# A two-layer graph attention kernel: one weight sum loaded ahead of the next weights, and three products with attention vectors moved into the second product's stage

## The chip, the cores and the metric

The kernel runs on one core of a Trainium2 chip. The core has five engines with an instruction queue each: TensorE (PE, matrix products into PSUM; its weight loads are shown as PEld), VectorE (DVE), ScalarE (ACT), GpSimd (POOL) and SyncE (SP). In this kernel SP does no arithmetic, it issues DMA transfers; GpSimd issues the transfers that add to their destination. Every queue is worked off in the order in which it was written. The metric is the device time of one execution in microseconds; lower is better.

## The reference

The reference is two graph attention layers, a residual and a layer norm over 512 nodes with 768 features. The first layer has 8 heads of 768 features, the second has one. Cut to what matters:

```
def gat_layer(x, W, a_s, a_d, b, edge_index, concat):
    h = (x @ W).reshape(n, H, C)
    alpha_s = einsum('nhc,hc->nh', h, a_s)
    alpha_d = einsum('nhc,hc->nh', h, a_d)
    e = leaky_relu(alpha_s[src] + alpha_d[dst], 0.2)
    e = exp(e - segment_max(e, dst)[dst])
    alpha = e / (segment_sum(e, dst)[dst] + 1e-16)
    out = segment_sum(h[src] * alpha[:, :, None], dst)
    return out.reshape(n, H * C) + b

h = elu(gat_layer(x, W1, a_src1, a_dst1, b1, edges, True))     # 8 heads
out = layernorm(x + gat_layer(h, W2, a_src2, a_dst2, b2, edges, True))
```

## The kernel before, in words

The edge list becomes a 512 x 512 matrix of edge counts at the start. From then on each head of the first layer is dense: a projection of x with the head's 768 x 768 weights, a softmax over the counted edges, a product of the attention matrix with the projected features, elu, and at once the head's share of the second layer's projection ("the second product"), which is added up over the heads.

The loop `for h in range(H - 1)` (line 991) runs in each round, in this order:

- `mixed(h, ...)` (line 867): the attention product of head h. TensorE's instructions have line 889.
- `second(h, GA, B2)` (line 442, called at 1011): the second product of head h, by a scheme of seven products P1 to P7 instead of eight, each in two halves. TensorE's line is 364, the evacuations on VectorE are L459. The loop over n from 2 to 6 (lines 1032 to 1072) puts the softmax of head h+1 between the halves: `lift` on ScalarE (L572), `leak` (L576) and `rank` (L581) on VectorE, `weigh` (L791 to L797) on VectorE, `turn_out` (a copy on ScalarE, L812, and a transposing DMA on SP, L814) and `turn_in` (L817).
- the projection of head h+2. For h from 1 to 5 it is `by_thirds` (line 407), which cuts the matrices in 2 x 3 and 3 x 3 blocks and needs 15 products P0 to P14 of eight TensorE instructions each instead of 18. TensorE's line is 423. The order of the products is P8, P13, P9, P2, P4, P12, P6, P0, P1, P10, P5, P14, P11, P7, P3.

The 15 products read sums of blocks of x and sums of blocks of weights. Nine of the sums of x lie in SBUF all the time. Five (for P7, P1, P6, P3 and P14) lie in gT, which the mixed product overwrites in each head; they are stored in DRAM once (`xd`), and `reload_x` (line 947, L948) brings them back in one transfer of 1280 KB at the end of each second product. P6 is the first product in the order that reads them.

The weight sums are made in two ways. `load_thirds` (line 132) loads the weights and lets GpSimd's adding transfers make some sums; its inner function `rest` (line 157), which the loop knows as `rest_of_thirds`, makes the others: VectorE operations (L165) and one pair of transfers for P11. P11's sum is a load on SP's queue (L161) into one half of the tile w2t4 and an adding transfer on GpSimd's queue (L162) on top of it, 256 KB each.

w2t4 and w2t2 are used twice in each round. Before `rest_of_thirds` they hold what `attended(h)` (line 975) loads for head h: 128 rows of the last head's W2 and the attention vectors of the second layer. It returns three VectorE operations (L985), products of these rows with the vectors, summed along the rows: 768, 384 and 384 elements wide. The first two read both tiles, the third only w2t2. They must be done before P11's load may write to w2t4.

`load_w2(h + 1)` (line 175, `load_w` at 103) loads the second product's next weights: seven transfers on SP's queue (L108, L116) and two adding ones on GpSimd's (L109, L120) into w1t1, w10 and w11. VectorE builds two more sums from them (`right`, L356 and L357); L356 is in VectorE's queue at the end of the 15 products.

The order of every queue is written out by hand: what stands first in the program is first in its engine's queue. A transfer on SP's queue that waits holds up everything behind it there.

Of the kernel before, what the change touches and what calls it, by code (L numbers as in the profile page):

```python
# [36 lines left out]
def gat_pass(  # L37
# [48 lines left out]
    def row_bcast(ap_row):  # L86
        return bass.AP(tensor=ap_row.tensor, offset=ap_row.offset, ap=[[0, P], [1, D]])
# [84 lines left out]
    def load_w1(h, slot="w2"):  # L172
        return load_w(W1, h, slot, w1[:, h * D:(h + 1) * D])

    def load_w2(h, slot="w1"):
        return load_w(W2, h, slot, w2[h * D:(h + 1) * D, :])

    def load_a(h, a_s, a_d):
        A[h] = []
        for name, a in (("a_s", a_s), ("a_d", a_d)):  # L180
            v = wpool.tile([P, D], F32, name=name)
            nc.sync.dma_start(v, row_bcast(a))
            A[h].append(v)
# [155 lines left out]
    def left(aT, s):  # L339
        a11, a12 = aT[:, :HK, :HN], aT[:, HK:, :HN]  # L340
        a21, a22 = aT[:, :HK, HN:], aT[:, HK:, HN:]
        tt = nc.vector.tensor_tensor
        return dict(P1=a11, P2=a12, P3=s[:, 2], P4=a22, P5=s[:, 0], P6=s[:, 1], P7=a21), [
            lambda: tt(s[:, 0], a21, a22, op=ALU.subtract),
            lambda: tt(s[:, 1], s[:, 0], a11, op=ALU.subtract),
            lambda: tt(a21, a11, a21, op=ALU.subtract),
            lambda: tt(s[:, 2], a12, s[:, 1], op=ALU.add),
        ]
# [23 lines left out]
    def half_logits(h, t):  # L372
        return [lambda al=al, a=a, sign=sign: nc.vector.scalar_tensor_tensor(
            scr, HS[h][:, t, :], sign, a, op0=ALU.mult, op1=ALU.mult, accum_out=al[:, t:t + 1])
            for al, a, sign in zip(AL[h], A[h], (1.0, -1.0))]
# [182 lines left out]
    def row_out(h):  # L558

        turned = small.tile([P, SQ], F32, name="turned", bufs=1)  # L560
        nc.vector.transpose(turned, wide[:, h % 2, :])
        row = drows.tile([NT, P], F32, name="drow")
        for j in range(P // SQ):
            nc.sync.dma_start(row[:, j * SQ:(j + 1) * SQ], turned[j * SQ:j * SQ + NT, :])
        BC[h] = qpool.tile([P, N], F32, name="q")
        r = row[:, :]
        nc.sync.dma_start(BC[h], bass.AP(tensor=r.tensor, offset=r.offset, ap=[[0, P], [1, N]]))
# [379 lines left out]
    def reload_x():  # L947
        nc.sync.dma_start(gF[:, :RELOAD * 2 * TH], stored)  # L948
# [42 lines left out]
    for h in range(H - 1):  # L991
        if 0 < h < H - 2:
            B3, rest_of_thirds = load_thirds(h + 2)
        elif h:
            A[H] = []
            for j, a in ((2, a_src2[0]), (4, a_dst2[0])):
                v = wpool.tile([P, HK, HALF], F32, name=f"w2t{j}").rearrange("p k n -> p (k n)")[:, :D]
                nc.sync.dma_start(v, row_bcast(a))
                A[H].append(v)
            last_sum = load_w2(H - 1, "w2")  # L1000
        GA, gsums = left(gT, gS)
        halves = [half_logits(h + 1, t) for t in ((0, 1) if h else (0, 1, 3))]
        besides[2:2] = [s_ for s_, _ in halves] + [lambda: row_out(h + 1)]
        finish = mixed(h, AA, BB, besides + [d_ for _, d_ in halves] + behind)
        besides, behind = [], []
        if h == 0:
            load_w1(2)()
        if h + 2 < H:
            load_a(h + 2, a_src1[h + 2], a_dst1[h + 2])
            attend = attended(h)  # L1010
        pairs = second(h, GA, B2)
        for m, _ in pairs[:2]:
            m()
        pairs[0][1]()
        for f in finish:
            f()
        gsums[0]()
        pairs[1][1]()
        gsums[1]()
        if pending:  # L1020
            pending.pop(0)()
        pairs[2][0]()
        gsums[2]()
        pairs[3][0]()
        gsums[3]()
        if pending:
            pending.pop(0)()
        pairs[2][1]()
        pairs[3][1]()
        last = h + 2 == H  # L1030
        q = [lift(h + 1, 0)]
        for n in range(2, 7):
            (m0, e0), (m1, e1) = pairs[2 * n:2 * n + 2]
            m0()
            if not last:
                m1()
            if n < 6:
                leak(q[n - 2])
                rank(q[n - 2], n - 2)
            if n < 5:  # L1040
                q.append(lift(h + 1, n - 1))
            if last:

                if n > 4:
                    turn_in(n - 5)
                if n == 6:
                    turn(q[2], 2)
                if n == 6:
                    weigh(q[3], 3)
                m1(lambda: turn(q[3], 3) if n == 6 else None)  # L1050
            if not last and n == 6:
                turn_in(0)
                weigh(q[2], 2)
                turn_out(q[2], 2)
            e0()
            if last and 2 < n < 6:
                weigh(q[n - 3], n - 3)
                if n < 5:
                    turn_out(q[n - 3], n - 3)
            if not last and 3 < n < 6:  # L1060
                weigh(q[n - 4], n - 4)
                turn_out(q[n - 4], n - 4)
            if not last and n == 6:
                weigh(q[3], 3)
                turn_out(q[3], 3)
                if 0 < h:
                    reload_x()
                load_w2(h + 1)()
            e1()
            for f in in_second[:1]:  # L1070
                f()
            del in_second[:1]
        if 0 < h and h + 2 < H:
            for f in attend:
                f()
            sums = rest_of_thirds()
            pairs = by_thirds(h + 2, XB, B3)
            AA, sums3 = left_sums(h + 1)
            B2, sums2 = right(W2[h + 1], "w1")
            for n in range(15):  # L1080
                pairs[n][0]()
                for p in {0: ("P6", "P2"), 1: ("P4",), 4: ("P10",), 5: ("P0",), 6: ("P1",), 9: ("P7",),
                          12: ("P3",)}.get(n, ()):
                    sums[p]()
                if n == 5:
                    BB, rsums_ = right_sums()
                    sums3 += rsums_
                if n in (2, 3, 5, 6, 8, 9, 10):
                    for _ in range(2 if n == 8 else 1):
                        sums3.pop(0)()  # L1090
                if n in (11, 13):
                    logits(h + 2, HS[h + 2], 2 + (n - 11) // 2)
                if n == 14:
                    sums2[0]()
                    behind = sums2[1:]
                pairs[n][1]()
                if n in (1, 2, 4):
                    turn_in((n + 2) // 2)
            assert not sums3
        elif h + 2 < H:  # L1100
            B_, sums = right(W1[h + 2], "w2")
            pairs = projection(h + 2, XA, B_)
            for n in range(14):
                pairs[n][0]()
                if n == 0:
                    for f in attend:
                        f()
                    B2, sums2 = right(W2[h + 1], "w1")
                if n in (1, 3):
                    sums[n // 2]()  # L1110
                if n == 1:
                    AA, sums3 = left_sums(h + 1)
                pairs[n][1]()
                if n in (1, 2, 4):
                    turn_in((n + 2) // 2)
                if n == 5:
                    BB, sums3 = right_sums()
                if 1 <= n < 9:
                    sums3.pop(0)()
                if n == 0:  # L1120
                    XB, early, again_, store, late_ = x_thirds()
                if n in (2, 4, 6, 8, 9):
                    early.pop(0)()
                if n == 9:
                    store()
                if n == 9:
                    again_()
                if n == 12:
                    late_.pop(0)()
                    sums2.pop(0)()  # L1130
                    behind = sums2 + late_[:2]
                    in_second = late_[2:]
                if n in (11, 13):
                    logits(h + 2, HS[h + 2], 2 + (n - 11) // 2)
        else:
            last_sum()
            B2, sums2 = right(W2[H - 1], "w1")
# [162 lines left out]
```

## Time and profile before

| | |
|---|---|
| median of 3 runs | 676.59 us (674.71 to 676.74) |
| the profiled execution | 677.39 us, its span 675.6 us |
| mean granted TensorE clock | 0.973 |
| DMA moved | 109.87 MB, mean 163 GB/s |
| TensorE, VectorE, ScalarE, GpSimd busy | 641.9, 537.9, 289.9, 63.6 us |

The profile is one execution, taken by the hardware profiler. Its times run from the span's start. A line such as L423 is the kernel's line of an instruction; the tile names stand without their buffer numbers, so w2t is w2t1, w2t2 or w2t4, and w is w10 or w11. "SPq" and "POOLq" are the queues that issue transfers. A row of the instructions in order of time has the start, the duration, engine, line, operation, output and input tiles, shapes and a count, and in brackets how long the engine stood idle before it and what ended that. Durations of TensorE's rows overlap a little with the next start, since its instructions are pipelined. A row of a table by stretches has the stretch, its length, the engine's busy time with the number of instructions, the clock granted to TensorE as a share of full speed, the mean busy share of the DMA engines and the GB/s they moved.

### The profile page before, as it was taken

Reading aid. Unit: us, or ns where it says so; the run is one execution under the profiler, and the core shown is the slowest. Engines: PE = TensorE matmul, PEld = TensorE weight load, DVE = VectorE, ACT = ScalarE, POOL = GpSimd, SP = SyncE. Lnnn points to the kernel's source line nnn. Section 1 sums busy time; section 2 is a strip of 40 time slices with the busy share of each in tenths; the row PEclk is TensorE's granted clock in tenths of the full one; section 3 lists DMA queues with packets and bytes.
Section 4 is the critical chain, followed back from the end, with each engine's and each line's share of the span. In section 5 each row is a group of like instructions: output and inputs, shape, how many; then the busy total and the mean of one; then the engine's idle time right before and its main releaser. Section 6 shows DMA issues by size and latency. Waiting matters only on the chain.

```text
span 675.6 us, 7677 instructions
## 1 busy us (share of the span) xinstructions
PE 641.9 (95%) x2509; PEld 445.3 (66%) x2509; DVE 537.9 (80%) x1162; ACT 289.9 (43%) x486; POOL 63.6 (9%) x105
## 2 busy tenths in 40 slices
PE   8999999999999799988999799997999889999996
PEld 5555685557668585777758686685857677544653
DVE  8989889979899578984889578885789758868685
ACT  5865564603544063611735035530636117443350
POOL 1300001012001020020200120010200210000000
PEclk9999999999999799997999899997999989999999
DMA  9993679697629483494907766294845955130031
GB/s 307 319 190 83 173 157 327 154 259 205 162 26 311 81 240 124 109 298 124 248 12 239 171 191 175 40 309 75 234 124 125 308 174 119 30 118 1 16 70 74
DMA packets 86844, 109.87 MB, mean 163 GB/s; under 512 B 40150, under 2 KB 67982, under 8 KB 86030
## 3 DMA queue, kind: packets, MB, share of 16 engines
q1 hardware_dynamic: 70590, 87.42, 40.9%
q0 software_dynamic: 15776, 21.30, 19.1%
q10 hardware_dynamic: 432, 0.59, 0.3%
q8 instruction: 22, 0.36, 0.2%
q14 instruction: 24, 0.20, 0.1%
HBM read 95.12 MB, written 2.90 MB: 145 GB/s over the span
## 4 chain that ended last, share of the span: by engine, by line
PE 86%; DMA 8%; DVE 2%; issue 1%; ACT 1%; SPq 0%; DVEq 0%; POOLq 0%; ACTq 0%
PE mm L364 41%; PE mm L889 18%; PE mm L423 14%; DMA w2t<-in_L_gnn_W_dram 7%; PE mm L835 3%; PE mm L1246 3%; PE held L364 2%; DMA gT<-xd 2%; PE tr L664 1%; PE held L544 1%; PE bc L233 1%; PE bc L664 0%; DVE scr L379 0%; ACT os L636 0%; PE mm L262 0%
## 5 line engine op out<-in xcount | busy, mean ns | idle before, releaser
L364 PE MATMUL mm<-w,gT 128*128 128x384 f32 x252 | 83.6, 486 | 0.0
L429 ACT ACTIVATE hs<-mm 128x512 f32<-128x512 f32 x30 | 17.9, 597 | 128.3 <-PE mm L423 110.3
L364 PEld LDWEIGHTS mm<-w,gT 128*128 128x128 f32 x252 | 47.9, 190 | 31.9
L431 DVE TENSOR_TENSOR hs<-hs,mm 128x512 f32<-128x512 f32 x45 | 30.8, 685 | 43.4 <-PE mm L423 43.3
L583 ACT ACTIVATE q<-q,nmax 128x512 f32<-128x512 f32 x36 | 25.8, 721 | 89.5 <-DVE nmax L581 89.5
L889 PE MATMUL mm<-PT,hs 128*128 128x256 f32 x252 | 61.3, 379 | 0.0
L364 PE MATMUL mm<-w1t,gS 128*128 128x384 f32 x180 | 60.6, 487 | 0.0
L423 PE MATMUL mm<-w2t,xS 128*128 128x256 f32 x120 | 37.7, 469 | 23.1 <-DMA w2t<-in_L_gnn_W_dram 23.1
L889 PEld LDWEIGHTS mm<-PT,hs 128*128 128x128 f32 x252 | 47.8, 190 | 7.3 <-issue 0.4
L364 PEld LDWEIGHTS mm<-w1t,gS 128*128 128x128 f32 x180 | 34.1, 190 | 24.1 <-DVE w1t L356 0.5
L459 DVE TENSOR_TENSOR h<-h,mm 128x384 f32<-128x384 f32 x72 | 39.1, 550 | 12.0 <-PE mm L364 11.5
L423 PEld LDWEIGHTS mm<-w2t,xS 128*128 128x128 f32 x120 | 27.8, 236 | 29.7 <-issue 24.9
L889 PE MATMUL mm<-pS,gS 128*128 128x256 f32 x168 | 43.2, 380 | 0.0
L423 PE MATMUL mm<-w2r,gT 128*128 128x256 f32 x160 | 40.8, 407 | 0.0
L817 ACT COPY PT<-zr 128x1024 uint16<-128x1024 uint16 x34 | 39.3, 1156 | 2.6 <-DMA zr<-pS 1.9
L423 PE MATMUL mm<-w2r,xT 128*128 128x256 f32 x160 | 37.8, 379 | 0.0
L423 PEld LDWEIGHTS mm<-w2r,gT 128*128 128x128 f32 x160 | 33.8, 211 | 5.9
L889 PEld LDWEIGHTS mm<-pS,gS 128*128 128x128 f32 x168 | 31.8, 190 | 4.7 <-DVE pS L862 0.4
L109 POOL DMA_DIRECT2D w1t<-in_L_gnn_W_dram x7 | 8.9, 1271 | 272.0 <-DVE hs L852 130.7
L812 ACT COPY pS<-q 128x1024 uint16<-128x1024 uint16 x26 | 27.2, 1044 | 17.0 <-DVE q L797 17.0
L423 PEld LDWEIGHTS mm<-w2r,xT 128*128 128x128 f32 x160 | 30.4, 190 | 5.2
L364 PE MATMUL mm<-w1t,gT 128*128 128x384 f32 x96 | 32.3, 486 | 0.0
(233 smaller groups left out, 1268.7 us busy)
## 6 DMA issues: line engine op xcount, KB each, us to landing
w2r<-in_L_gnn_W_dram SPq DMA_DIRECT2D x48, 384.0 KB, 8.9
w<-in_L_gnn_W_dram SPq DMA_DIRECT2D x43, 384.0 KB, 10.0
gT<-xd SPq DMA_DIRECT2D x5, 1280.0 KB
w1t<-in_L_gnn_W_dram SPq DMA_DIRECT2D x9, 576.0 KB
w<-in_L_gnn_W_dram POOLq DMA_DIRECT2D x8, 576.0 KB, 9.5
w1t<-in_L_gnn_W_dram POOLq DMA_DIRECT2D x7, 576.0 KB, 9.6
w2t<-in_L_gnn_W_dram SPq DMA_DIRECT2D x15, 256.0 KB, 7.5
w2t<-in_L_gnn_W_dram POOLq DMA_DIRECT2D x15, 256.0 KB, 8.9
```

The source lines that it names most:

```text
L109: nc.gpsimd.dma_start(t1, upper[:, :, R], accum_op=ALU.add)
L364: nc.tensor.matmul(ps[:, :HALF], A_[p][:, k, i * P:(i + 1) * P], B_[p][:, k, :], start=start and k == 0, stop=k == HK - 1, skip_group_chec ...
L423: nc.tensor.matmul(bank[chain][:, i * TH:(i + 1) * TH], A_[p][:, k, i * P:(i + 1) * P], B_[p][:, k, :], start=first and i == k == 0, stop= ...
L429: nc.scalar.activation(out(o), ps, AF.Copy, scale=how)
L431: nc.vector.tensor_tensor(out(o), out(o), ps, op=how)
L459: nc.vector.tensor_tensor(a, a, ps, op=ALU.subtract if p == "P7" else ALU.add)
L583: nc.scalar.activation(q, q, AF.Exp, bias=nmax, scale=-1.0)
L812: nc.scalar.copy(apart.rearrange("p (h n) -> p h n", h=2), q.bitcast(U16).rearrange("p (n h) -> p h n", h=2))
L817: nc.scalar.copy(PT.rearrange("p s n -> p (s n)").bitcast(U16).rearrange("p (s n h) -> p s n h", s=NT, h=2)[:, :, t * P:(t + 1) * P, :], p ...
L835: nc.tensor.matmul(ps[:, :N], HS[h][:, s, c * P:(c + 1) * P], PT[:, s, :], start=(s == 0), stop=(s == NT - 1))
L889: nc.tensor.matmul(bank[p][:, :HN], A_[p][:, k, c * P:(c + 1) * P], B_[p][:, k, :], start=over is None and k == 0, stop=k == 1, skip_group ...
L1246: nc.tensor.matmul(ps[:, :cols.stop - cols.start], PT[:, s, t * P:(t + 1) * P], h2[:, s, cols], start=(s == 2), stop=(s == 1))
```

## The change

Two things move, and both only for h from 1 to 5, the rounds with 15 products.

`rest_of_thirds()`, which issues P11's load on SP's queue and its adding transfer on GpSimd's and returns the VectorE sums, was called after the second product's loop. It is now called in the loop's last step (n = 6), after the last `turn_out` and before `reload_x()` and `load_w2(h + 1)`. The VectorE sums that it returns are placed as before.

The three operations of `attended(h)`, which were placed together after the loop, are now placed one each at the end of the steps n = 3, 4 and 5, behind the second evacuation `e1`.

```
                 turn_out(q[3], 3)
                 if 0 < h:
+                    sums = rest_of_thirds()
                     reload_x()
                 load_w2(h + 1)()
             e1()
             for f in in_second[:1]:
                 f()
             del in_second[:1]
+            if 0 < h and not last and 2 < n < 6:
+                attend[n - 3]()
         if 0 < h and h + 2 < H:
-            for f in attend:
-                f()
-            sums = rest_of_thirds()
             pairs = by_thirds(h + 2, XB, B3)
```

On SP's queue the order at the end of a second product was: four transposing transfers, the reload of gT (L948), seven weight loads (L108, L116), P11's load (L161). It is now: four transposing transfers, P11's load, the reload, the seven weight loads. On GpSimd's queue it was L109, L120, L162 and is now L162, L109, L120. TensorE's and ScalarE's queues are the same in both, and so are the number of instructions and the bytes.

## The prediction

> **What bounds the kernel now.** I read the page first (busy shares and the chain that ended last), then who waited for whom, then TensorE's instructions in order of time in one head.
>
> ```profile
> span 675.6 us, 7677 instructions
> PE 641.9 (95%) x2509; PEld 445.3 (66%) x2509; DVE 537.9 (80%) x1162; ACT 289.9 (43%) x486; POOL 63.6 (9%) x105
> ...
> PE 86%; DMA 8%; DVE 2%; issue 1%; ACT 1%; SPq 0%; DVEq 0%; POOLq 0%; ACTq 0%
> PE mm L364 41%; PE mm L889 18%; PE mm L423 14%; DMA w2t<-in_L_gnn_W_dram 7%; PE mm L835 3%; PE mm L1246 3%; PE held L364 2%; DMA gT<-xd 2%; PE tr L664 1%; PE held L544 1%; PE bc L233 1%; PE bc L664 0%; DVE scr L379 0%; ACT os L636 0%; PE mm L262 0%
> ```
>
> TensorE is busy 95% of the span and 86% of the chain. The only large item beside it is a transfer into w2t, the tile whose weight sum this change moves. The list of waits says how often TensorE really stands for it, and the rows of one head (the second of the five 15-product projections) say where; their columns are start and duration in us, and in brackets the idle time before.
>
> ```profile
> PE mm L423 <- DMA w2t<-in_L_gnn_W_dram: 23.1, 5, 4.9
> ```
>
> ```profile
> 297.76 1.89 PE L423 MATMUL mm<-w2r,xS 128*128 128x256 f32 x8
> 299.48 1.89 PE L423 MATMUL mm<-w2r,gT 128*128 128x256 f32 x8
> 305.80 3.75 PE L423 MATMUL mm<-w2t,xS 128*128 128x256 f32 x8 [4.43 <-DMA w2t<-in_L_gnn_W_dram]
> ...
> 313.66 1.03 PE L889 MATMUL mm<-PT,hs 128*128 128x256 f32 x4
> ```
>
> One product of eight matmuls normally starts 1.72 us after the one before (299.48 - 297.76). The 13th product, P11, comes at 305.80 instead of 301.21. It happens once in each of five heads. The second loss stands in the same rows: P11, P7 and P3 then take 7.86 us (305.80 to 313.66), where three pitches make 5.18. Stretches of these three products, first and last of the five and their sum (length, TensorE busy, granted clock, DMA share, GB/s):
>
> ```profile
> 227.03:235.02 7.99, 7.99 (x24) 0.65 0.00 0
> ...
> 542.21:549.63 7.42, 7.42 (x24) 0.70 0.30 74
> sum 38.76, PE 38.76; mean PE 7.75
> ```
>
> The granted clock is 0.65 to 0.70 there: the wait throttles TensorE, and it pays for that afterwards.
>
> **The change, part by part.** Removed, if P11's sum is there in time: the wait, 23.1 us plus five times the 0.16 by which a row's end overlaps the next start (1.89 - 1.73) = 23.9 us; and the slow clock, 38.76 - 5 x 5.18 = 12.9 us. Together 36.8 us, 7.4 a head. That is the most that it can bring.
>
> Is the sum in time? The two transfers of P11 (a load on SP's queue, then an adding one from GpSimd), and those around them:
>
> ```profile
> 280.95 1.05 ACT L812 COPY nr<-q 128x1024 uint16<-128x1024 uint16 x1 [0.88 <-DVE q L797]
> ```
> ```profile
> 282.02 1.23 SPq L814 DMA_TRANSPOSE zr<-nr  x1
> 283.36 0.52 SPq L948 DMA_DIRECT2D gT<-xd  x1
> 283.98 0.38 SPq L108 DMA_DIRECT2D w1t<-in_L_gnn_W_dram  x1
> 284.45 3.02 SPq L116 DMA_DIRECT2D w<-in_L_gnn_W_dram  x6
> 289.45 0.38 SPq L161 DMA_DIRECT2D w2t<-in_L_gnn_W_dram  x1
> ```
> ```profile
> 291.52 1.28 POOL L109 DMA_DIRECT2D w1t<-in_L_gnn_W_dram  x1 [42.47 <-PE mm L423]
> ...
> 301.25 1.22 POOL L162 DMA_DIRECT2D w2t<-in_L_gnn_W_dram  x1 [5.51 <-DVE hs L431]
> ```
> ```profile
> gT<-xd SPq DMA_DIRECT2D x5, 1280.0 KB
> w1t<-in_L_gnn_W_dram POOLq DMA_DIRECT2D x7, 576.0 KB, 9.6
> w2t<-in_L_gnn_W_dram SPq DMA_DIRECT2D x15, 256.0 KB, 7.5
> w2t<-in_L_gnn_W_dram POOLq DMA_DIRECT2D x15, 256.0 KB, 8.9
> ```
>
> Now P11's load is issued at 289.45, behind the reload and seven weight loads, and its add only at 301.25. In the changed order the load is the first thing behind the last transpose. Its issue time is the reload's old one plus whatever delays the transpose, at most the 2.07 us found below: 285.43. With the medians from issue to landing (7.5 and 8.9 us) the sum is there by 301.8, and P11 wants it at 301.21 plus whatever the product is delayed elsewhere (1.9 us, below). So even with the medians under load the wait goes; the load has less ahead of it, so I expect some 297.
>
> What moves on VectorE: the three products with attention vectors, 768, 384 and 384 wide.
>
> ```profile
> 269.08 0.56 DVE L459 TENSOR_TENSOR h<-h,mm 128x384 f32<-128x384 f32 x1 [1.38 <-PE mm L364]
> ...
> 281.30 0.95 DVE L985 SCALAR_TENSOR_TENSOR scr<-w2t,w2t 128x768 bf16<-128x768 f32 x1
> ...
> 282.29 0.56 DVE L985 SCALAR_TENSOR_TENSOR scr<-w2t,w2t 128x384 bf16<-128x384 f32 x1
> ...
> 282.78 0.55 DVE L985 SCALAR_TENSOR_TENSOR scr<-w2t 128x384 bf16<-128x384 f32 x1
> ...
> 283.37 0.69 DVE L165 TENSOR_TENSOR w2t<-w2r 128x512 f32<-128x512 f32 x1
> ```
> ```profile
> 269.55:283.37 13.82, 13.22 (x39) 1.00 0.32 60
> ```
>
> They take 281.30 to 283.37, 2.07 us. They go behind the evacuations of steps 3, 4 and 5 of the second product. VectorE's last wait for TensorE there ends at 269.08, and from 269.55 to 283.37 it is busy 13.22 of 13.82 us. So nothing absorbs them: the work behind each comes 1.0, 1.6 and 2.07 us later, while the weight sums from L165 on start when they do now. Banks and softmax steps have room, but the last weighing of q (L797) ends 2.07 us later, and behind it hang ScalarE's copy at 280.95, the transpose at 282.02 and all of SP's queue. That is the price: P11's load and then the reload of gT issue late.
>
> How much room has the reload? P11's load waits for the reload's landing today, so its issue time dates that landing; P6, the seventh product, is the first that reads the reloaded gT. First and last of the five heads, and the second:
>
> ```profile
> SPq L161 <- DMA gT<-xd: 8.8, 5, 1.9
> ```
> ```profile
> 211.06 0.38 SPq L161 DMA_DIRECT2D w2t<-in_L_gnn_W_dram  x1
> ```
> ```profile
> 211.85 1.89 PE L423 MATMUL mm<-w2t,gT 128*128 128x256 f32 x8
> ```
> ```profile
> 290.85 1.89 PE L423 MATMUL mm<-w2t,gT 128*128 128x256 f32 x8
> ```
> ```profile
> 525.13 0.39 SPq L161 DMA_DIRECT2D w2t<-in_L_gnn_W_dram  x1
> ```
> ```profile
> 526.78 1.89 PE L423 MATMUL mm<-w2t,gT 128*128 128x256 f32 x8
> ```
>
> The room is 0.79, 1.40 and 1.65 us; I use 1.2. Against it stand 2.07 us from VectorE, and P11's load ahead in the queue. That load costs at least its issue, 0.5 us (0.38 and a gap), and by its bytes a fifth of the reload's 6.1 us (289.45 - 283.36): 1.2. I take 1.0, nearer to the bytes since both go through one queue. So the reload lands 3.07 us later and P6 stands 1.9 us, 9.3 in five heads. The low bound is (2.07 + 0.5 - 1.2) x 5 = 6.8. P11's add (4.55 us from its issue at 301.25 to P11's start at 305.80) may also run beside the reload's end; at half rate for 1 to 2 us it adds up to 1 us a head, so the high bound is 14. Nothing below zero is possible there, because a load put ahead cannot bring the reload forward.
>
> Does this stall throttle TensorE too? Three stretches of 3.41 us: the one that ends where the clock fell in the fifth head, the one behind it, and one early in the kernel with a gap in which it did not fall:
>
> ```profile
> 536.39:539.80 3.41, 0.91 (x5) 1.00 1.12 254
> 539.80:543.21 3.41, 1.00 (x3) 0.50 0.46 72
> ```
> ```profile
> 14.13:17.54 3.41, 2.29 (x28) 1.00 1.06 386
> ```
>
> A stretch of 3.41 us with 0.91 us of work was followed by half clock; one with 2.29 us of work was not. A stall of 1.9 us leaves 1.5 us of work if it falls into one stretch, between the two. A fall costs what it costs now, 12.9/5 = 2.6 us; I put one head in four: 3.2 us, bounds 0 and 13. The Trainium skill (TensorE: Matmul & The Clock Gate, "The HAM clock gate") says that the clock falls after an idle window of about 3.4 us and that the window runs freely. By that this stall would cost no clock and the result would be 3 us lower. The trace agrees on the length of the window, not on its being idle: here 0.91 us of work did not save it. So the rows decide.
>
> Late next: GpSimd now does P11's add before the add into w1t (L109). The latter waits for its own plain load, which lands some 3.1 us later like the reload, so it issues near 294.6 and, with 9.6 us, lands near 304.2. Its reader:
>
> ```profile
> 312.74 1.35 DVE L356 TENSOR_TENSOR w1t<-w1t,w 128x1152 f32<-128x1152 f32 x1
> ```
>
> This comes about 5 us earlier when P11 does not wait: 312.74 - 7.4 + 1.9 = 307.2, still 3 us behind the data. If that cover were gone, VectorE would hold the first additions of the mixed products, and TensorE with them. I cost it at nothing.
>
> **Sum.** The profiled execution took 677.39 us, 1.79 more than its span and 0.80 above the median of the runs. 677.39 - 36.8 + 9.3 + 3.2 = 653.1; against the median 652.3.
>
> **The rivals.** (1) The reload is not late enough to matter: P6 stalls little and all 36.8 us come: 640. For it: the reload has 0.8 to 1.65 us of room. Against it: a fully busy VectorE and SP's single file. (2) The reload comes later still, and TensorE's clock falls in every head: stall 2.7 and 2.6 for the clock, 5 x 5.3 = 26.5, giving 666. For it: the add runs while the reload does. The Trainium skill (DMA: Bandwidth & Descriptors, "Queues, rings and completion order") has each DMA engine take turns between the rows of GpSimd's and SP's transfers, which speaks for that sharing; no row here shows this pair side by side. (3) Slower: the reload effectively starts only when P11's load has landed. With 7.5 us for that load, P6 stands 2.07 + 7.5 - 1.2 = 8.4 us, plus 2.6 of clock, 11.0 a head: 676.6 - 36.8 + 55 = 695. It decides once stall and clock pass 7.4 us a head, that is, from a reload 6.0 us late. For it: the median. Against it: SP's row of six weight loads takes 3.02 us together, so one transfer doesn't wait there for the landing of the one before. (4) The change does not do what it says: P11's add still lands late beside the reload, P6's stall is only taken off P11's, and the time stays near 676.
>
> **How the numbers follow.** Chances: forecast 0.60, (1) 0.13, (2) 0.18, (3) 0.05, (4) 0.04. Faster by over 0.3% (about 2 us, what this measurement can tell) is the forecast, (1) and (2): 0.91; same 0.04; slower 0.05. The range runs from (1), half of which it holds, to a little past (2): 640 to 667; outside lie (3), (4) and half of (1), 0.16.
>
> **What would show it.** In the list of waits TensorE's 23.1 us for w2t should be gone and a new wait for gT at P6, five times 1.3 to 2.8 us, should stand there. The last three products should take 5.2 us at clock 1.00. SP should issue P11's load near its 285.4 equivalent, right behind the transpose. VectorE's L985 should sit between L459 and L576. Wrong: no wait at P6 (then VectorE's delay was hidden), a clock of 0.5 behind P6, or an idle VectorE ahead of L356.

## The result, and the profile after

| | before | after |
|---|---|---|
| median | 675.65 us (674.60 to 676.74, 4 runs) | 647.41 us (646.83 to 647.88, 4 runs) |
| the profiled execution, its span | 677.39 us, 675.6 us | 647.71 us, 645.9 us |
| mean granted TensorE clock | 0.973 | 0.999 |

The ratio is 0.9581, with a 95% interval of 0.9559 to 0.9604: the change saves about 28 us. The page of the changed kernel, its busy times and its chain of waits:

```profile
span 645.9 us, 7667 instructions
PE 630.7 (98%) x2509; PEld 434.9 (67%) x2509; DVE 535.4 (83%) x1162; ACT 289.8 (45%) x486; POOL 63.6 (10%) x105
...
PE 88%; DMA 5%; DVE 4%; ACT 1%; issue 1%; DVEq 0%; SPq 0%; ACTq 0%
PE mm L364 41%; PE mm L889 19%; PE mm L423 15%; DMA gT<-xd 5%; PE mm L835 3%; PE mm L1246 3%; PE held L364 2%; PE tr L664 1%; PE bc L233 1%; PE held L544 1%; PE bc L664 0%; DVE h L459 0%; ACT os L636 0%; DVE scr L379 0%; PE mm L262 0%
```

TensorE's 2509 matmuls take 11.2 us less (641.9 before): that is the slow clock, which shows as 11.6 us in the stretches below. The page counts ten instructions fewer in all, but each engine's own count is the same as before. The transfer into w2t is gone from the chain, and the reload of gT, with SP's and VectorE's work ahead of it, stands there instead. What TensorE waits for now, in the list of waits (total us, times, longest):

```profile
PE mm L423 <- DMA gT<-xd: 4.2, 5, 1.1
...
PE mm L364 <- DVE h L459: 1.1, 1, 1.1
```

The wait for w2t (23.1 us) is away; a wait for gT came, once in each of the five heads, and one for VectorE's evacuations in the first of them. TensorE's rows in the same head as before, from the 6th product to the end:

```profile
283.08 1.89 PE L423 MATMUL mm<-w2t,xS 128*128 128x256 f32 x8
285.77 1.96 PE L423 MATMUL mm<-w2t,gT 128*128 128x256 f32 x8 [0.79 <-DMA gT<-xd]
...
294.48 1.89 PE L423 MATMUL mm<-w2r,gT 128*128 128x256 f32 x8
296.20 1.89 PE L423 MATMUL mm<-w2t,xS 128*128 128x256 f32 x8
298.08 3.72 PE L423 MATMUL mm<-w2r,gT 128*128 128x256 f32 x16
301.64 1.03 PE L889 MATMUL mm<-PT,hs 128*128 128x256 f32 x4
```

P11 now starts one pitch behind the product before it (296.20 - 294.48 = 1.72). P11, P7 and P3 take 5.44 us instead of 7.86. The same stretches in the first and the last head and their sum, with the granted clock in the column behind the busy time:

```profile
223.38:228.82 5.44, 5.44 (x26) 1.00 0.72 125
...
514.60:520.03 5.43, 5.43 (x25) 1.00 1.12 242
sum 27.18, PE 27.18; mean PE 5.44
```

From the first mixed product of one head to that of the next, the chain's steps give 78.65 us before (235.18 to 313.83) and 72.82 us after (228.98 to 301.80): 5.8 us a head.

### The profile page after: what moved, and what is told of

The parts are those of the page before. It is cut to its first block, busy times and chain, and to the rows that moved or that the text cites. A ratio compares the mean times of both kernels' runs of the same rounds, so it can differ in the third digit from the quotient of the medians.

```text
span 645.9 us, 7667 instructions
## 1 busy us (share of the span) xinstructions
PE 630.7 (98%) x2509; PEld 434.9 (67%) x2509; DVE 535.4 (83%) x1162; ACT 289.8 (45%) x486; POOL 63.6 (10%) x105
## 4 chain that ended last, share of the span: by engine, by line
PE 88%; DMA 5%; DVE 4%; ACT 1%; issue 1%; DVEq 0%; SPq 0%; ACTq 0%
PE mm L364 41%; PE mm L889 19%; PE mm L423 15%; DMA gT<-xd 5%; PE mm L835 3%; PE mm L1246 3%; PE held L364 2%; PE tr L664 1%; PE bc L233 1%; PE held L544 1%; PE bc L664 0%; DVE h L459 0%; ACT os L636 0%; DVE scr L379 0%; PE mm L262 0%
## 5 line engine op out<-in xcount | busy, mean ns | idle before, releaser
L429 ACT ACTIVATE hs<-mm 128x512 f32<-128x512 f32 x30 | 17.9, 596 | 91.6 <-PE mm L423 91.2
L459 DVE TENSOR_TENSOR h<-h,mm 128x384 f32<-128x384 f32 x72 | 39.0, 549 | 11.8 <-PE mm L364 11.5
L431 DVE TENSOR_TENSOR hs<-hs,mm 128x512 f32<-128x512 f32 x45 | 30.8, 684 | 21.3 <-PE mm L423 21.3
L423 PE MATMUL mm<-w2r,gT 128*128 128x256 f32 x160 | 37.5, 382 | 0.0
L423 PEld LDWEIGHTS mm<-w2r,gT 128*128 128x128 f32 x160 | 30.0, 190 | 5.8 <-DVE hs L431 1.9
L364 PE MATMUL mm<-w,gS 128*128 128x384 f32 x84 | 29.3, 495 | 1.1 <-DVE h L459 1.1
L638 DVE TENSOR_SCALAR os<-nodes,idx 128x512 bf16<-128x512 f16 x104 | 29.0, 352 | 1.4 <-PE tr L664 1.4
L893 ACT COPY u<-mm 128x256 f32<-128x256 f32 x21 | 7.8, 372 | 49.2 <-PE mm L889 49.2
```

The lines of the kernel that those rows point to most:

```text
L364: nc.tensor.matmul(ps[:, :HALF], A_[p][:, k, i * P:(i + 1) * P], B_[p][:, k, :], start=start and k == 0, stop=k == HK - 1, skip_group_chec ...
L423: nc.tensor.matmul(bank[chain][:, i * TH:(i + 1) * TH], A_[p][:, k, i * P:(i + 1) * P], B_[p][:, k, :], start=first and i == k == 0, stop= ...
L429: nc.scalar.activation(out(o), ps, AF.Copy, scale=how)
L431: nc.vector.tensor_tensor(out(o), out(o), ps, op=how)
L459: nc.vector.tensor_tensor(a, a, ps, op=ALU.subtract if p == "P7" else ALU.add)
L638: nc.vector.tensor_scalar(o, nodes, idx[:, c:c + 1], None, op0=ALU.is_equal)
```

## The experiments

Each run is compared with runs of the kernel before on the same chip (medians 675.22 us for the first four, 675.52 us for the others; 675.65 us for the change itself, so differences between these groups are uncertain by some 0.4 us). All diffs but that of the run without P11's sum are against the changed kernel.

**Only the products moved.**

```
                 if 0 < h:
-                    sums = rest_of_thirds()
                     reload_x()
...
         if 0 < h and h + 2 < H:
+            sums = rest_of_thirds()
             pairs = by_thirds(h + 2, XB, B3)
```

> Only the products with attention vectors are moved; P11's load and add keep their old place behind the weights. Theory (the load's place brings the gain, the products' place only costs): SP's queue runs about 1.5 us later against TensorE than before, P11's sum lands that much later, TensorE waits about 6 us for it in each of five heads and the clock still falls: 675.65 + 5 x 1.5 = 683 us, slower than before. Rival (the moved products bring a part of the gain themselves, because VectorE's weight sums start earlier): at or below 675 us.

Measured: 683.93 us (683.72 to 684.47), ratio 1.0127 [1.0110, 1.0144]. The list of waits:

```profile
PE mm L423 <- DMA w2t<-in_L_gnn_W_dram: 27.4, 5, 6.1
PE mm L423 <- DMA gT<-xd: 1.8, 3, 1.0
```

Moving the products alone makes the kernel slower by 8.7 us: everything on SP's queue comes later, P11's sum too. The whole gain belongs to the other half of the change.

**The reload ahead of P11's load.**

```
-                    sums = rest_of_thirds()
                     reload_x()
+                    sums = rest_of_thirds()
```

> The changed kernel with the reload of gT ahead of P11's load on SP's queue. Theory (the wait at P6 is room 1.3 us against a delay of some 1.5 us from VectorE and 0.8 us from P11's load): without the load ahead the wait falls from 1.0 to about 0.2 us a head, so 647.4 - 5 x 0.8 = 643.4 us, and P11's sum is still in time. Rival A (only VectorE's delay counts): no change, 647 us. Rival B (P11's sum has no room to spare): the wait comes back at P11, 647 us or more.

Measured: 645.05 us (643.83 to 646.12), ratio 0.9543 [0.9527, 0.9560], 1.7 us above what was expected and 2.4 us below the changed kernel. So P11's load ahead of the reload costs about 0.5 us a head. The wait at P6 did not go everywhere: the list has 1.2 us for gT in three heads and 1.2 us at P6 in a fourth, which it puts down to VectorE (the evacuation L431 of the product before). P6 does not need that evacuation: in the second head of the changed kernel it starts at 285.77, while the same evacuation runs (285.43 to 286.11). In the fourth head the reload was issued at 423.14 and P6 started at 430.56, 7.4 us later, against 6.0 to 6.7 in the first three. That the reload itself took longer there is my reading of it; the trace doesn't date its landing.

**The products in VectorE's waits.**

```
+            if 0 < h and not last and n in (2, 3):
+                for f in (attend[:1] if n == 2 else attend[1:]):
+                    f()
             e1()
...
-            if 0 < h and not last and 2 < n < 6:
-                attend[n - 3]()
```

> The changed kernel with the three products placed where VectorE stands for TensorE in the second product: the first ahead of the second evacuation of step 2, the other two ahead of that of step 3, into two waits of 1.38 us each. Theory (VectorE's delay of SP's queue makes the wait at P6): the last transpose issues some 1.5 us earlier against TensorE, the reload is late only by P11's load (0.8 us against 1.3 us of room), the wait for gT is gone and the small waits for L459 too: 647.4 - 5 x 1.0 - 1.5 = 641 us. Rival (the load's 256 KB make it): the wait at P6 stays near 1 us, 646 to 647 us.

Measured: 642.39 us (641.68 to 642.58), ratio 0.9511 [0.9495, 0.9527], 1.4 us above what was expected. VectorE's rows in the second head show how the waits take them in:

```profile
255.81 0.95 DVE L985 SCALAR_TENSOR_TENSOR scr<-w2t,w2t 128x768 bf16<-128x768 f32 x1
...
257.27 0.56 DVE L459 TENSOR_TENSOR u<-u,mm 128x384 f32<-128x384 f32 x1 [0.50 <-PE mm L364]
...
260.16 0.55 DVE L985 SCALAR_TENSOR_TENSOR scr<-w2t 128x384 bf16<-128x384 f32 x1
...
261.14 0.56 DVE L459 TENSOR_TENSOR h<-h,mm 128x384 f32<-128x384 f32 x1 [0.42 <-PE mm L364]
```

The two waits of 1.38 us shrink to 0.50 and 0.42 us and nothing behind them moves. The reload is issued 3.45 us behind the first of the 15 products (276.00 - 272.55), in the changed kernel 4.90 us (279.35 - 274.45). The wait for gT is 0.9 us in one head and none in the other four, though P11's load is still ahead of the reload. So VectorE's delay, by way of SP's queue, is the larger part of that wait, and P11's load the smaller.

**The products twice.**

```
                 attend[n - 3]()
+                attend[n - 3]()
```

> The changed kernel with each of the three products done twice in its place (the same sums are written twice). Theory (one us on VectorE there is one us at P6): VectorE and SP's queue come about 1.8 us later, the wait for gT grows from 0.8 to about 2.7 us, 647.4 + 5 x 1.8 = 656.5 us if TensorE's clock stays at 1.00. If a gap of 2.7 us already throttles it, up to 2.6 us more a head, 660 to 669 us, and stretches at 0.5 behind P6. Rival (the delay is absorbed somewhere): 647 to 650 us.

Measured: 659.02 us (657.97 to 661.84), ratio 0.9770 [0.9745, 0.9796]. The sum is near what was expected, but not by the way that was expected:

```profile
PE mm L364 <- DVE h L459: 8.5, 5, 2.7
PE mm L423 <- DMA gT<-xd: 2.6, 2, 1.6
PE mm L423 <- DVE hs L431: 2.5, 2, 1.2
```

```profile
268.43 4.03 PE L364 MATMUL mm<-w1t,gS 128*128 128x384 f32 x12
273.91 4.19 PE L364 MATMUL mm<-w,gS 128*128 128x384 f32 x12 [1.45 <-DVE h L459]
```

Most of VectorE's further delay appears inside the second product. Its last product P3 is added up in P5's bank and so waits for P5's evacuation (L459), which stands behind the moved products. What TensorE has lost there, the reload has gained, so the wait at P6 hardly grows: 5.1 us against 4.2, with the two waits that the list puts down to L431 and that are the reload's, as above. VectorE needs 15.57 us in the second head from the first product to the first weight sum (265.23 to 280.80), 13.37 us in the changed kernel (263.35 to 276.72): 2.2 us more, 11.0 in five heads. The time grew by 11.6 us. In that lies one fall of the clock, behind the wait of 2.66 us in the first head, some 1.7 us by my estimate (a step of 3.4 us at half clock, last section). So a microsecond on VectorE costs about one, but at the first place where TensorE needs VectorE.

**The products behind, P11 between reload and weights.**

```
                 if 0 < h:
-                    sums = rest_of_thirds()
                     reload_x()
-                load_w2(h + 1)()
+                else:
+                    load_w2(h + 1)()
...
-            if 0 < h and not last and 2 < n < 6:
-                attend[n - 3]()
         if 0 < h and h + 2 < H:
+            for f in attend:
+                f()
+            sums = rest_of_thirds()
+            load_w2(h + 1)()
```

> The three products are back behind the second product's loop, as before the change; SP's order is reload, P11's load (which waits for the products), weights. Theory (the gain is P11's place ahead of the weights; nothing need be paid for it at P6): the reload issues as before the change, no wait for gT, P11's load lands right behind the reload and its add, 9.1 us from issue in the changed kernel, is ready about 20 us after the first product, where P11 wants it at 20.7: 675.2 - 36.8 = 638 us, up to 641 us if the add is a little late. Rival A (VectorE's relief by the moved products is a part of the gain): 643 us or more with waits for L165. Rival B (no room for the add): a wait for w2t at P11 comes back, 645 us or more.

Measured: 641.54 us (640.75 to 641.70), ratio 0.9495 [0.9478, 0.9512]; 0.5 us above the upper end of what was expected. The list of waits has none for gT or w2t. So the products need not move at all: the place behind the reload and ahead of the weights is early enough for P11. It differs from the run with the reload first only in where the products stand, and that is 645.05 - 641.54 = 3.5 us.

**No sum for P11** (diff against the kernel before).

```
-            B_.update(P6=square(two, 0), P2=square(two, 1), P11=square(four, 0), P10=square(four, 1))
-            nc.sync.dma_start(B_["P11"], part(0, 1))
-            nc.gpsimd.dma_start(B_["P11"], part(1, 1), accum_op=add)
+            B_.update(P6=square(two, 0), P2=square(two, 1), P11=raw[0, 1], P10=square(four, 1))
```

> The kernel before with P11's load and add left out; P11 reads the block of P5 instead, so that sum is not computed. This measures what the wait and the slow clock behind it cost together. Theory: 23.9 us of waiting and 12.9 us of half clock go, 675.2 - 36.8 = 638.4 us, and the clock stays at 1.00 in the five stretches of P11, P7 and P3. Rival (the clock's loss has another cause than the wait): the wait goes but those stretches stay slow, 651 us.

Measured: 642.12 us (641.72 to 642.38), ratio 0.9506 [0.9489, 0.9522], 3.7 us above what was expected; mean clock 0.999. The wait and what hangs on it cost 33.4 us by the medians and 35.0 us by the profiled executions (677.39 - 642.38). The slow clock goes with the wait, so it has no other cause here.

**The products in the waits and the reload first.**

```
-                    sums = rest_of_thirds()
                     reload_x()
+                    sums = rest_of_thirds()
...
+            if 0 < h and not last and n in (2, 3):
+                for f in (attend[:1] if n == 2 else attend[1:]):
+                    f()
             e1()
...
-            if 0 < h and not last and 2 < n < 6:
-                attend[n - 3]()
```

> The products in VectorE's two waits, as in the run that put them there, and the reload ahead of P11's load. Theory: beside 642.4 us only the one wait for gT left there (0.9 us in the first of the five heads) can go: 641 to 642 us. Rival (P11's add becomes late, since its load now issues behind the reload): a wait for w2t at P11, 643 us or more.

Measured: 640.54 us (640.26 to 641.10), ratio 0.9484 [0.9467, 0.9500], a little lower than was expected. No wait for gT or w2t is left. This version beats both kernels, the changed one by 6.9 us.

**The reload behind the first weight load.**

```
-                    reload_x()
-                load_w2(h + 1)()
+                load_w2(h + 1, then=reload_x if 0 < h else None)()
```

`then` is called in `load_w` right after the load of t1 (L108).

> The changed kernel with the reload of gT put one place further back on SP's queue, behind the first weight load of 576 KB. Theory by bytes (transfers of one queue are served in turn): the reload issues 0.5 us later and lands 1.7 to 2.2 us later, the wait for gT grows from 0.8 to some 2.7 us a head; without a slower clock 647.4 + 5 x 2.0 = 657 us, with the clock falling in every head up to 670 us. Theory by issue alone (the transfers run side by side): 0.5 us a head, 650 us.

Measured: 666.52 us (664.30 to 673.18), ratio 0.9884 [0.9833, 0.9934]. TensorE's waits at P6 in the first and last head (this kernel's lines are numbered two higher):

```profile
215.18 2.48 PE L425 MATMUL mm<-w2t,gT 128*128 128x256 f32 x8 [3.61 <-DMA gT<-xd]
```
```profile
522.01 1.96 PE L425 MATMUL mm<-w2t,gT 128*128 128x256 f32 x8 [3.18 <-DMA gT<-xd]
```

The five gaps are 3.61, 3.05, 3.20, 2.71 and 3.18 us, 2.3 us more a head than in the changed kernel (15.75/5 - 4.2/5). That is the price by bytes; by issue alone it would have been 0.5. The list puts the gap of 2.71 us down to VectorE (L855); the reload was issued 7.8 us ahead of P6 there, against 8.1 to 8.3 in the other heads. The rest of the loss (17.9 us by the profiled executions, less 11.6 of waiting) is the clock, which fell in four of the five heads (last section).

## Why the prediction was right

Predicted were 652.3 us (640 to 667) and faster; measured 647.41. The terms as they came out add up: 677.39 - 35.0 (wait and slow clock) + 4.2 (wait at P6) + 1.1 (wait in the second product) = 647.7, and the profiled execution took 647.71. The mechanism was right; the misses partly cancel, since the gain was put 1.8 us too high, the stall and its clock 8.3 us too high, and 1.1 us was not foreseen. Each step:

- The wait and its slow clock, forecast 36.8 us. The wait went as forecast. The last three products fell from 38.76 to 27.18 us, not to 25.9: when P11 does not wait, P7 starts 0.15 us late (298.08 - 296.20 - 1.73) and P7 and P3 take 3.56 instead of 3.45 (301.64 - 298.08). The run without P11's sum shows 35.0 us as the possible gain, 1.8 less than forecast; this rest is 1.3 of it.
- P11's sum is in time. Its load was issued at 278.84 in the second head, behind the last transpose, and its add 3.7 us later:

```profile
282.51 1.20 POOL L162 DMA_DIRECT2D w2t<-in_L_gnn_W_dram  x1 [39.32 <-DMA w2t<-in_L_gnn_W_dram]
```

  Before the change that took 11.8 us (289.45 to 301.25): SP issued the load only when the reload had landed, and the chain has 10.96 us from there to the load's own landing, behind seven weight loads. The add now lands 9.1 us after its issue, at 291.6, which is 17.2 us behind the first product (274.45) where 16.5 was forecast (297 - 280.49), and 4.6 us ahead of P11. TensorE has no wait for w2t. Every run moved the load and the add together or neither; what the add's new place on GpSimd's queue brings alone is not shown.
- The products cost VectorE 2.07 us and delay SP's queue by as much: right in kind, too large. Counted from the first of the 15 products, the last transpose was issued at 1.53 us before (282.02 - 280.49) and at 2.99 us after (277.44 - 274.45, TensorE's row of that product begins at 274.45), 1.46 us later. In their new place each costs less:

```profile
263.35 0.95 DVE L985 SCALAR_TENSOR_TENSOR scr<-w2t,w2t 128x768 bf16<-128x768 f32 x1
264.22 0.08 DVE L985 DVE_READ_ACCUMULATOR scr<-w2t,w2t 128x1 f32 x1
264.22 0.69 DVE L576 SCALAR_TENSOR_TENSOR q<-q 128x512 f32<-128x512 f32 x1
...
268.01 0.55 DVE L985 SCALAR_TENSOR_TENSOR scr<-w2t,w2t 128x384 bf16<-128x384 f32 x1
268.49 0.08 DVE L985 DVE_READ_ACCUMULATOR scr<-w2t,w2t 128x1 f32 x1
268.49 0.69 DVE L576 SCALAR_TENSOR_TENSOR q<-q 128x512 f32<-128x512 f32 x1
```

  The work behind starts 0.87 and 0.48 us later, not 1.0 and 0.6, since it runs while the sum is read out. So the last weighing of q ends 1.62 us later, counted from the evacuation ahead of the first product (269.08 and 262.88): 0.2 of the 1.83 went into VectorE's own short waits. TensorE's 15 products begin 0.16 us later, counted in the same way, which leaves 1.46.
- P11's load ahead of the reload, taken as 1.0 us. Issue to issue it is 0.51 us:

```profile
277.44 1.23 SPq L814 DMA_TRANSPOSE zr<-nr  x1
278.84 0.46 SPq L161 DMA_DIRECT2D w2t<-in_L_gnn_W_dram  x1
279.35 0.48 SPq L948 DMA_DIRECT2D gT<-xd  x1
```

  The chain of waits has the reload at 6.28 us (279.35 to 285.63) in this head, 6.03 before: 0.25 more, 0.76 together. The 0.25 is one head's figure: over the five heads of the changed kernel the reload took 5.99 to 6.52 us. Nothing in these rows calls for a price of P11's add beside it, but no run tests that alone.
- The wait at P6, forecast as 9.3 us, is the term that was mis-sized: 4.2 us stand in the list. Delay and room were both read right in kind; 1.46 + 0.76 - 1.3 is 0.9 us a head, where 2.07 + 1.0 - 1.2 was forecast. (The 1.3 is this head's room, 290.85 - 289.39 less the 0.14 from landing to start.)
- The clock at P6, forecast as 3.2 us: nothing. The mean clock is 0.999; the gaps are 1.1 us at most.
- L356, costed at nothing: it runs at 301.62 directly behind the evacuation before it. The list of waits has none for it.
- Not forecast: VectorE's delay also holds P3 of the second product, 1.06 us in the first head, where VectorE has further work in that loop, and about 0.2 in the others. That banks and softmax steps have room was the sentence that failed. It was small here; the run with the products twice shows what it can become.

The rivals: no late reload (640 us) is what the runs with the reload first and the products out of the way show, 640.5 and 641.5. A clock that falls in every head (666 us) needed a reload 2.3 us later still. A reload that only starts once P11's load has landed is excluded by 6.28 us from issue to landing. A stall at P6 that is only taken off P11's (676 us) is excluded by the missing wait for w2t. So the change as made is two parts of unlike value: by subtraction of medians, the load's place brings 675.5 to 641.5, the moved products give back 3.5 us and the load's place ahead of the reload instead of behind it another 2.4.

## What to carry to other kernels

When a transfer in a queue is late, look at what stands ahead of it and who needs each of them first; here it had only to pass the weights, which are needed after it, not the reload, which is needed before it. Freeing a buffer earlier is not free if the engine that frees it also feeds the queue: put such work into a wait of that engine, or leave it, if the later place is early enough. A wait of TensorE that is long enough to throttle it costs more than its own length: here 11.6 us of slow clock came on top of 23.9 us of waiting.

## What the runs showed of the hardware

The granted clock does not fall by the length of the gap alone. In the run with the reload behind the first weight load, a gap of 2.71 us was followed by half clock and one of 3.18 us was not. The falls lie on a grid: they were read at 216.50, 291.59, 370.09 and 445.19, which are 22, 23 and 22 steps of 3.413 us apart. TensorE's busy time in steps of that grid, four that end with a fall and the two that share the last gap:

```profile
213.09:216.50 3.41, 1.32 (x6) 1.00 1.03 310
288.18:291.59 3.41, 0.72 (x4) 1.00 0.99 372
366.68:370.09 3.41, 1.41 (x7) 1.00 1.04 302
441.78:445.19 3.41, 0.70 (x4) 1.00 0.97 402
516.87:520.28 3.41, 1.96 (x10) 1.00 0.97 345
520.28:523.69 3.41, 1.68 (x8) 1.00 1.06 300
```

Steps with up to 1.41 us of work were followed by half clock, steps with 1.68 us or more were not. This takes it that a step ends where the fall is recorded; if it ends some tenths of a microsecond earlier, the bound moves with it. By these six steps a gap may be 1.7 us in any place without a fall (3.41 - 1.68), and up to 3.18 us where the grid's edge cuts it in two. It would also explain the spread of that run (664.30 us at a mean clock of 0.990 to 673.18 us at 0.978), if the grid lies otherwise in each execution; that was not tried. In the prediction 1.5 us of work was left between the two bounds, and these steps put the bound between 1.41 and 1.68. The Trainium skill (TensorE: Matmul & The Clock Gate, "The HAM clock gate") has the window's length, about 3.4 us, and that it runs freely; the measured grid agrees with both. That a fall needs an idle window does not hold here: steps 41% busy were followed by one.

How long the clock stays low follows the same grid. In that run it lasted about one step of 3.4 us in each of the four heads, and TensorE was back before the step began or at most 0.36 us into it. Before the change it lasted two in each of the five heads (225.75 to 232.58 in the first); there TensorE resumed 1.3 to 2.4 us into the first step (at 227.03 in the first head). That the clock rises behind the first step which TensorE nearly fills is my reading of these nine cases.
